# Placing query-projection pieces, two stray tiles and a ring's slots in a latent-attention kernel

## The chip, the cores and the metric

One core of a Trainium2 chip runs the whole kernel. The metric is device time in microseconds (us) of one execution; the time before is the median of 3 runs. The engines are named as in the profile: PE (TensorE, matrix products), DVE (VectorE), ACT (ScalarE), POOL (GpSimd) and SP (SyncE, which here only issues DMAs). They run side by side, each through its own queue in order, and wait for one another through semaphores.

## The reference

One layer over 2048 tokens of width 512: multi-head latent attention with 16 heads, a residual and a layer norm, then one linear layer with a second residual and norm.

```
cq   = rms_norm(x @ w_qa.T)                      # 384 wide
q    = cq @ w_qb.T                               # 16 heads, 128 nope + 64 pe
q_pe = q_pe * cos + rotate_half(q_pe) * sin
ckv  = x @ w_kva.T                               # 128 latent + 64 pe
k_pe = rope(ckv[128:]);  kv = rms_norm(ckv[:128]) @ w_kvb.T   # k_nope, v
s    = (q . k) * 192**-0.5, causal
out  = softmax(s) @ v @ w_o.T
x    = layernorm(x + out);  x = layernorm(x + x @ (w * scale).T + bias)
```

## The kernel before

Everything that enters a product in float32 is split into a high part h and a rest l, so that three products of the fast kind (hh, hl, lh) stand for one exact product. The key projection is folded into the query weights, and values are taken from the 128-wide latent itself.

The queries are four blocks b of 512 rows. A block has eight pairs p of heads, a pair has four query tiles qt of 128 rows, and a tile has two heads j. In blocks 1 to 3 a pair thus has eight head steps, numbered 2 * qt + j, from 0 to 7. The keys of a tile are nk = (4b + qt + 1) * 128, so steps get longer with qt and b.

One head step (`head_scores`, `head_probs`) is a chain over the engines. PE forms the scores s into PSUM (L407: three products with Kn, two with Kp). DVE adds the mask (L413), takes the row maximum (L440) and makes the bias (L447, L449). ACT takes the exponential into pr (L455). DVE inverts the sums; ACT writes the high half of the probabilities hl (L476) and DVE the rest (L479). SP issues a DMA that transposes hl into the ring (L483). From there PE multiplies with the latent (`values`, L532), in two halves per tile. This product is called PV in the text. ACT copies its result into ot (L537), which SP sends to memory (L292).

PSUM holds the scores in pool "s" (three buffers in blocks 1 and 3, two in block 2, which has a small pool "t" beside it) and everything else in pool "m", two buffers in turn: PV results and projection pieces. Each block has its own score pools, on the same banks.

The queries of the next pair are made in pieces between the steps: `project_pe` has two pieces of nine products (L334), one for each half x of the rope dimensions, after which DVE multiplies with cos and sin (L339), POOL combines (L346, L347), ACT rounds (L349, the tile ph), and sixteen small operations lay out pe (L358 or L360, and L361). `project_nope` has two pieces (L377), each followed by a split on ACT and DVE (L66, L67). `project_pe` serves two pairs, so pairs with even p carry four pieces (for a later pair) and those with odd p two. The weights have one buffer each: `load_wq` and `load_wpe` are issued on SP right after the last piece that reads the buffer, and must wait for it.

In blocks 1 to 3 the orders of PE and SP are the program's own; the other engines' orders come from a scheduler. A step is written as: scores of this head with the probabilities of the head before it between them, then `fill()` where a piece is due (it takes the next one from the list `fillers`), then `run_values(lag)`, which does PV halves of tiles that are far enough behind. Which steps have a piece is decided here:

```
early = b == 1 and p + 1 < NPAIR
if j != early or qt == 0 and (early or b == 2 and p > 0):
    fill()
```

The ring is 24576 columns wide. `room` finds a place for a tile's transposed probabilities: it looks only at slots of equal size, 2048 * (b + 1) columns, and while none is free it does PV halves of the oldest tiles. Block 0's last tile lies in a tile of its own, named carry, and its PV is done at step 0 of pair (1,0), by two calls of `half_values`.

After block 3 comes the output part (L775 and later), which the change leaves as it is.

Of the kernel before, what the change touches and what calls it, by code (L numbers as in the profile page):

```python
# [9 lines left out]
F16 = mybir.dt.float16  # L10
# [9 lines left out]
P = 128  # L20
# [5 lines left out]
NB = 4  # L26
QB = 512
NPAIR = H // 2
# [21 lines left out]
def mla_block(ctx: ExitStack, tc: tile.TileContext, a, out):  # L50
# [6 lines left out]
    def move(queue, dst, src):  # L57
        queue.dma_start(dst.bitcast(F32), src.bitcast(F32))
# [53 lines left out]
    prj = ctx_p.enter_context(tc.tile_pool(name="prj", bufs=1, side="right"))  # L112
# [59 lines left out]
    def value_output(p, wvo, wv, wo, pool, tag):  # L172

        for j in range(2):
            ps = pool.tile([P, HID], F32, tag=tag, name=f"ps_wo{2 * p + j}")
            nc.tensor.matmul(ps, wv[j], wo[j], start=True, stop=True)  # L176
            split(ps, wvo[:, 0, j, :], wvo[:, 1, j, :], kvln_o)
            yield
# [109 lines left out]
    def put_in(all=False):  # L288
        kept = []
        for n, dst, src in later:  # L290
            if n == 0 or all:
                nc.sync.dma_start(dst, src)  # L292
            else:
                kept.append([n - 1, dst, src])
        later[:] = kept
# [20 lines left out]
    def load_wpe(b, g):  # L316
        if b == NB:
            return
        w = state["wpe", b, g] = prj.tile([P, 2, LT, 256], F32R, tag="wpe", name=f"wpe{b}_{g}")
        move(state["queue"], w, wpe_d[g])  # L320

    def project_pe(b, g, direct=None):

        if direct is None and ("wpe", b, g) not in state:
            load_wpe(b, g)
        w = state.pop(("wpe", b, g)) if direct is None else direct
        cq, cs = state["cq"], state["cs"]
        prod = prj.tile([P, 2, 2, QB], F32, tag="prod", name=f"prod{b}_{g}")
        for x in range(2):
            ps = psum["m"].tile([P, QB], F32, tag="m", name=f"ps_pe{b}_{g}_{x}")  # L330
            n = 0
            for lt in range(LT):
                for i, k in ((0, 0), (0, 1), (1, 0)):
                    nc.tensor.matmul(  # L334
                        ps, w[:, i, lt, x * P : (x + 1) * P], cq[:, k, lt, :], start=n == 0, stop=n == 8
                    )
                    n += 1
            for k in range(2):
                nc.vector.tensor_tensor(prod[:, k, x, :], ps, cs[:, k ^ x, :], ALU.mult)  # L339
            if x:  # L340
                if b or g == 3:
                    load_wpe(*((b, g + 1) if g < 3 else (b + 1, 0)))
            yield
        rp, tp = prod[:, 0], prod[:, 1]
        eng = nc.vector if (b, g) == (0, 0) else nc.gpsimd
        eng.tensor_tensor(rp[:, 0, :], rp[:, 0, :], rp[:, 1, :], ALU.subtract)  # L346
        eng.tensor_tensor(rp[:, 1, :], tp[:, 0, :], tp[:, 1, :], ALU.add)  # L347
        ph = prj.tile([P, 2, QB], F32R, tag="ph", name=f"ph{b}_{g}")
        nc.scalar.activation(ph, rp, AF.Copy)  # L349
        pe = blk.tile([P, 4, QB], F32R, tag="pe", name=f"pe{b}_{g}")  # L350

        quick = b == 0 or g == 0
        for j in range(4):
            q = slice(32 * j, 32 * j + 32)
            for x in range(2):
                to = pe[32 * x : 32 * x + 32, j, :]
                if quick:
                    nc.scalar.activation(to, rp[q, x, :], AF.Copy)  # L358
                else:
                    nc.gpsimd.tensor_copy(to, rp[q, x, :])  # L360
                (nc.gpsimd if not quick or (b, g) == (0, 0) and j % 2 else nc.vector).tensor_tensor(  # L361
                    pe[64 + 32 * x : 96 + 32 * x, j, :], rp[q, x, :], ph[q, x, :].bitcast(F32), ALU.subtract
                )
        state["pe", b, g] = pe

    def project_nope(b, p, direct=None):
        if direct is None and ("wq", b, p) not in state:
# [22 lines left out]
    def project(b, p):  # L390
        if p % 2 == 0:
            yield from project_pe(b, p // 2)
        yield from project_nope(b, p)
# [191 lines left out]
    for _ in project_pe(0, 0, wpe0):  # L585
        pass
# [13 lines left out]
    probs, vals = [], []  # L600

    def flush():
        while probs:
            for _ in probs.pop():
                pass

    def units(pool, ring, b):
        lag = min(ring.shape[1] // (2048 * (b + 1)) - 1, 3)

        for p in range(NPAIR):  # L610
            put_in(True)
            if b and p % 2 == 0 and p + 2 < NPAIR:
                fillers.append(project_pe(b, p // 2 + 1))
            if p + 1 < NPAIR:
                fillers.append(project(b, p + 1) if b == 0 else project_nope(b, p + 1))
            elif b + 1 < NB:
                fillers.append(project(b + 1, 0))
            if b == NB - 1 and p == NPAIR - 2:
                wv = state["wv"] = blk.tile([P, H, P], F32, tag="pe", name="wv")
                nc.sync.dma_start(wv, a["wv"])  # L620
                wo = state["wo"] = [pool.tile([P, 4, HID], F32, tag="wo", name="wo0", bufs=1)]
                nc.sync.dma_start(wo[0], a["wo"][:, 0:4])
            if b == NB - 1 and p == NPAIR - 1:
                ctx_p.close()
                pcr = state["pcr"] = ctx.enter_context(
                    tc.tile_pool(name="pcr", bufs=2, side="right", reuse_waits="tile")
                )
                wvo = state["wvo"] = [pcr.tile([P, 2, 2, HID], F32R, name=f"wvo{p}", bufs=1) for p in range(2)]
                wv, wo = state["wv"], state["wo"]
                for i in range(2):  # L630
                    fillers.append(
                        value_output(
                            i, wvo[i], [wv[:, 2 * i + j] for j in range(2)], [wo[0][:, 2 * i + j] for j in range(2)],
                            psum["m"], "m",
                        )
                    )
                wo.append(blk.tile([P, 4, HID], F32, tag="qn", name="wo1"))
                nc.sync.dma_start(wo[1], a["wo"][:, 4:8])
            for qt in range(4):
                nk = (4 * b + qt + 1) * P  # L640
                if (b, p, qt) == (0, NPAIR - 1, 3):
                    s0, PT = -4 * nk, prj.tile([P, 4 * nk], F16, tag="prod", name="carry")
                else:
                    s0 = room(2048 * (b + 1), ring.shape[1])
                    PT = ring[:, s0 : s0 + 4 * nk]
                vg = values(b, p, qt, nk, PT)
                if nk <= 512:
                    pi = pair_scores(pool, b, p, qt, nk)
                    flush()
                    probs.append(pair_probs(pool, b, p, qt, nk, PT, *pi))  # L650
                    fill()
                    next(side[0], None)
                    if p and qt % 2:
                        next(side[1], None)
                    if qt % 2:
                        next(side[0], None)
                    run_values(lag)
                    run_values(lag)
                else:
                    for j in range(2):  # L660
                        prev = probs.pop() if probs else iter(())
                        pi = head_scores(pool, b, p, j, qt, nk, prev)
                        probs.append(head_probs(pool, b, p, j, qt, nk, PT, *pi))
                        if (b, p, qt, j) == (1, 0, 0, 0):
                            half_values()
                            half_values()
                        early = b == 1 and p + 1 < NPAIR
                        if j != early or qt == 0 and (early or b == 2 and p > 0):
                            fill()
                        run_values(lag)  # L670
                vals.append([vg, 0, s0, s0 + 4 * nk])
            drain()
# [7 lines left out]
    def run_values(depth):  # L680

        for _ in range(1 + len(vals) - depth):
            half_values()

    def room(n, size):

        while True:
            for c in range(0, size - n + 1, n):
                if all(c + n <= v[2] or c >= v[3] for v in vals):
                    return c  # L690
            if len(vals) == 1:
                flush()
            half_values()
# [20 lines left out]
    ring = blk13.tile([P, 12 * 2048], F16, name="ring", bufs=1)  # L714
# [202 lines left out]
```

## Time and profile before

| | |
|---|---|
| median of 3 runs | 1661.89 us (1661.62 to 1665.02) |
| profiled execution | 1661.02 us, its span 1659.2 us |
| mean granted TensorE clock | 0.981 |
| PE busy | 1567.8 us, 94% |
| DVE busy | 1172.6 us, 71% |
| ACT busy | 936.1 us, 56% |
| POOL busy | 330.7 us, 20% |
| block 1's first scores / end of block 3 | about 257 us / 1393 us from the start |
| pair (1,3), pair (2,3), pair (3,3) | 30.7, 42.8, 58.1 us |

A row of the list of waits reads: who waited, for whom, us in total, how many times, the longest. A row of a stretch reads: start and end, length, busy time of each engine with its number of instructions, granted TensorE clock, share of the time that the DMA engines were busy, GB/s. A row of the timeline reads: start, duration, engine, line, operation, output and inputs, number merged, and in brackets the idle time before it with what ended it. A row of a group of instructions ends in its busy time, the mean in ns, and the engine's idle time before it.

### The profile page before, as it was taken

Reading aid. Unit: us, or ns where it says so; the run is one execution under the profiler, and the core shown is the slowest. Engines: PE = TensorE matmul, PEld = TensorE weight load, DVE = VectorE, ACT = ScalarE, POOL = GpSimd, SP = SyncE. Lnnn points to the kernel's source line nnn. Section 1 sums busy time; section 2 is a strip of 40 time slices with the busy share of each in tenths; the row PEclk is TensorE's granted clock in tenths of the full one; section 3 lists DMA queues with packets and bytes.
Section 4 is the critical chain, followed back from the end, with each engine's and each line's share of the span. In section 5 each row is a group of like instructions: output and inputs, shape, how many; then the busy total and the mean of one; then the engine's idle time right before and its main releaser. Section 6 shows DMA issues by size and latency. Waiting matters only on the chain. (4 is left out here: it accounts for less than half of the span.)

```text
span 1659.2 us, 24718 instructions
## 1 busy us (share of the span) xinstructions
PE 1567.8 (94%) x9130; PEld 1299.4 (78%) x9130; DVE 1172.6 (71%) x2115; ACT 936.1 (56%) x1647; POOL 330.7 (20%) x404
## 2 busy tenths in 40 slices
PE   8998997999998799999998999999999997999997
PEld 7787876778777678888887888888888785788886
DVE  6777776777777868787786777767767774455464
ACT  5776765565556646666675656666566664312120
POOL 2332424143100505040000310500500000022132
PEclk9999998999999999999999999999999998999999
DMA  6979674878787767878887677787688998333230
GB/s 218 246 213 238 156 194 108 165 163 159 159 193 151 146 141 149 178 153 169 201 180 140 117 160 153 152 159 161 126 158 191 189 179 188 105 108 120 90 121 32
DMA packets 632841, 262.50 MB, mean 158 GB/s; under 512 B 570288, under 2 KB 611120, under 8 KB 631696
## 3 DMA queue, kind: packets, MB, share of 16 engines
q1 hardware_dynamic: 621184, 233.35, 64.7%
q0 software_dynamic: 4768, 17.99, 3.5%
q10 hardware_dynamic: 6768, 9.57, 1.9%
q8 instruction: 72, 1.18, 0.3%
q14 instruction: 49, 0.40, 0.1%
HBM read 83.17 MB, written 35.13 MB: 71 GB/s over the span
## 5 line engine op out<-in xcount | busy, mean ns | idle before, releaser
L407 PE MATMUL s<-Kn,qn 128*128 128x512 f32 (+4 forms) x1920 | 520.7, 377 | 12.2 <-ACT pr L455 10.3
L455 ACT ACTIVATE pr<-s,bias,rq 128x1024 f32<-128x1024 f32 (+3 forms) x320 | 324.1, 1016 | 194.2 <-DVE bias L449 150.4
L532 PE MATMUL o<-ring,V 128*128 128x256 f16 x3252 | 400.7, 277 | 27.7 <-DMA ring<-hl 18.2
L479 DVE SCALAR_TENSOR_TENSOR hl<-pr,inv,hl 128x1024 f16<-128x1024 f32 (+7 forms) x320 | 358.7, 1136 | 83.0 <-ACT hl L476 81.2
L532 PEld LDWEIGHTS <-V 128*128 128x128 f16 x3264 | 307.4, 99 | 117.6 <-issue 61.6
L476 ACT ACTIVATE hl<-pr,inv 128x1024 f16<-128x1024 f32 (+7 forms) x320 | 295.4, 961 | 182.6 <-DMA ring<-hl 74.9
L407 PEld LDWEIGHTS s<-Kn,qn 128*128 128x128 f32 x1920 | 338.7, 190 | 61.1 <-ACT pr L455 16.6
L440 DVE TENSOR_REDUCE neg<-s 128x1 f32<-128x1024 f32 (+3 forms) x320 | 318.5, 995 | 83.9 <-PE s L407 79.9
L407 PE MATMUL s<-Kp,pe 128*128 128x512 f32 (+4 forms) x1280 | 361.0, 363 | 0.0
L407 PEld LDWEIGHTS s<-Kp,pe 128*128 128x128 f32 x1280 | 234.0, 189 | 29.8
L377 PE MATMUL ps_qn<-cq,wq 128*128 128x512 f32 x576 | 151.9, 410 | 23.0 <-DMA wq<-wq_d 15.5
L346 POOL TENSOR_TENSOR prod<-prod 128x512 f32<-128x512 f32 x15 | 19.3, 1288 | 740.7 <-DVE prod L339 740.7
L377 PEld LDWEIGHTS ps_qn<-cq,wq 128*128 128x128 f32 x576 | 111.1, 198 | 47.6 <-issue 12.5
L775 PE MATMUL acc<-wvo,oh 128*128 128x512 f32 x448 | 143.5, 401 | 0.0
L361 POOL TENSOR_TENSOR pe<-prod,ph 32x512 fp32r<-32x512 f32 x76 | 119.7, 1575 | 10.0 <-issue 5.1
L775 PEld LDWEIGHTS acc<-wvo,oh 128*128 128x128 f32 x448 | 83.4, 188 | 20.9 <-issue 2.9
L775 PE MATMUL acc<-wvo,ol 128*128 128x512 f32 x224 | 88.4, 395 | 0.0
L284 POOL DMA_DIRECT2D ot_d<-ot x33 | 18.7, 568 | 293.8 <-ACT ot L537 263.1
L334 PE MATMUL ps_pe<-cq,wpe 128*128 128x512 f32 x288 | 73.2, 400 | 2.3 <-DMA cq<-cq_d 1.6
L537 ACT ACTIVATE ot<-o 128x256 f32<-128x256 f32 x128 | 48.0, 376 | 38.0 <-PE o L532 36.3
L63 ACT ACTIVATE oh<-o 128x1024 fp32r<-128x1024 f32 x28 | 29.6, 1058 | 67.6 <-PE acc L775 53.5
L64 DVE TENSOR_TENSOR ol<-o,oh 128x1024 fp32r<-128x1024 f32 x28 | 38.5, 1376 | 41.3 <-ACT oh L63 41.3
(140 smaller groups left out, 1624.3 us busy)
## 6 DMA issues: line engine op xcount, KB each, us to landing
wq<-wq_d SPq DMA_DIRECT2D x22, 768.0 KB, 5.6
o<-ot_d SPq DMA_DIRECT2D x32, 512.0 KB, 3.3
ot_d<-ot SPq DMA_DIRECT2D x95, 128.0 KB, 2.4
wpe<-wpe_d SPq DMA_DIRECT2D x10, 768.0 KB, 4.8
wq<-wq_d POOLq DMA_DIRECT2D x9, 768.0 KB, 6.2
wq_d<-wst SPq DMA_DIRECT2D x9, 512.0 KB, 4.7
cq_d<-cqst SPq DMA_DIRECT2D x18, 256.0 KB, 3.6
ot_d<-ot POOLq DMA_DIRECT2D x33, 128.0 KB, 2.6
```

The lines of the kernel that those rows point to most:

```text
L64: nc.vector.tensor_tensor(l, ps, h.bitcast(F32), ALU.subtract)
L334: nc.tensor.matmul(ps, w[:, i, lt, x * P : (x + 1) * P], cq[:, k, lt, :], start=n == 0, stop=n == 8)
L361: (nc.gpsimd if not quick or (b, g) == (0, 0) and j % 2 else nc.vector).tensor_tensor(pe[64 + 32 * x : 96 + 32 * x, j, :], rp[q, x, :], ph ...
L377: nc.tensor.matmul(ps, w[:, i, lt, j * P : (j + 1) * P], cq[:, k, lt, :], start=n == 0, stop=n == 8)
L407: nc.tensor.matmul(ps[:, :w], lhs, K[:, i, c0 : c0 + w], start=n == 0, stop=n == 4)
L440: nc.vector.tensor_reduce(neg[:, ti : ti + 1], v, axis=AX.XY, op=ALU.max, negate=True)
L455: nc.scalar.activation(pr[:, c0 : c0 + n * w].rearrange("p (a c) -> p a c", a=n), v, AF.Exp, bias=bias, scale=r, accum_out=sums[:, ti : ti ...
L476: nc.scalar.activation(hl[:, 0, c], pr[:, c], AF.Copy, scale=inv)
L479: nc.vector.scalar_tensor_tensor(hl[:, 1, c], pr[:, c], inv, hl[:, 0, c], ALU.mult, ALU.subtract)
L532: nc.tensor.matmul(ps[:, :256], vt[:, i, k % 4, :], v[:, :, l, k, :], start=n == 0, stop=n == 3 * kts - 1)
L537: nc.scalar.activation(ot, ps[:, :256], AF.Copy)
L775: nc.tensor.matmul(acc, l[:, t, c], wvo[p][:, i, j, :], start=p == 0 and j == 0 and n == 0, stop=p == NPAIR - 1 and j == 1 and n == 2,)
```

## The change

The steps that carry a piece become a table `at`: 0, 1, 3, 4 in pairs with four pieces (0, 1, 2, 3 in (1,0)), 3, 4 in pairs with two, 1, 2, 4, 5 in the last pair of blocks 1 and 2, and 1, 3, 5, 7 in the last pair of block 3. In `project_pe` the work after the products (combining, rounding, laying out) follows the second piece at once; before, it was done with the next piece. The laying out of pe for (2,0) and (3,0) goes from ACT and DVE to POOL, as that of the other groups of blocks 1 to 3. The carry tile takes the buffer of tag "ph" in place of "prod", and its PV is done at step 2 of (1,0). `room` may also place a tile right behind a live one, in just the width that it needs: when no slot is free, or first of all for the last three tiles of block 2.

```diff
@@ project_pe
             for k in range(2):
                 nc.vector.tensor_tensor(prod[:, k, x, :], ps, cs[:, k ^ x, :], ALU.mult)
-            if x:
-                if b or g == 3:
-                    load_wpe(*((b, g + 1) if g < 3 else (b + 1, 0)))
-            yield
+            if x == 0:
+                yield
+            elif b or g == 3:
+                load_wpe(*((b, g + 1) if g < 3 else (b + 1, 0)))
...
-        quick = b == 0 or g == 0
+        quick = b == 0 or (b, g) == (1, 0)
...
         state["pe", b, g] = pe
+        yield
@@ units
             put_in(True)
+            if p + 1 == NPAIR:
+                at = (1, 2, 4, 5) if b < NB - 1 else (1, 3, 5, 7)
+            elif p % 2 == 0 and p + 2 < NPAIR:
+                at = (0, 1, 2, 3) if (b, p) == (1, 0) else (0, 1, 3, 4)
+            else:
+                at = (3, 4)
...
-                    s0, PT = -4 * nk, prj.tile([P, 4 * nk], F16, tag="prod", name="carry")
+                    s0, PT = -4 * nk, prj.tile([P, 4 * nk], F16, tag="ph", name="carry")
                 else:
-                    s0 = room(2048 * (b + 1), ring.shape[1])
+                    s0 = room(2048 * (b + 1), ring.shape[1], 4 * nk, (b, p) == (2, NPAIR - 1) and qt > 0)
...
-                        if (b, p, qt, j) == (1, 0, 0, 0):
+                        if (b, p, qt, j) == (1, 0, 1, 0):
                             half_values()
                             half_values()
-                        early = b == 1 and p + 1 < NPAIR
-                        if j != early or qt == 0 and (early or b == 2 and p > 0):
+                        if 2 * qt + j in at:
                             fill()
@@ room
-    def room(n, size):
+    def room(n, size, need, dense):
         while True:
-            for c in range(0, size - n + 1, n):
-                if all(c + n <= v[2] or c >= v[3] for v in vals):
+            slots = [(c, n) for c in range(0, size - n + 1, n)]
+            gaps = [(c, need) for c in sorted([0] + [v[3] for v in vals]) if c + need <= size]
+            for c, w in gaps + slots if dense else slots + gaps:
+                if all(c + w <= v[2] or c >= v[3] for v in vals):
                     return c
```

## The prediction

> **What bounds the kernel now.** I read the page first, then TensorE's waits, then granted clock by stretch, then the timeline around the longest waits. TensorE (PE) is the bound: busy 94% of the span, with 91 us of idle. The change touches only the stretch from block 1's first scores (257 us) to the end of block 3 (1393 us), so I asked for PE's waits there (columns: total us, number of waits, longest):
>
> ```profile
> PE ps_qn L377 <- DMA wq<-wq_d: 15.0, 3, 11.5
> PE s L407 <- ACT pr L455: 10.3, 13, 2.3
> PE o L532 <- DMA ring<-hl: 8.5, 5, 4.3
> PE ps_qn L377 <- DVE qn L67: 5.0, 4, 2.3
> PE o L532 <- DMA carry<-hl: 5.0, 1, 5.0
> PE o L532 <- ACT ot L537: 3.8, 4, 2.7
> PE o L532 <- DVE prod L339: 0.9, 1, 0.9
> PE ps_pe L334 <- DVE prod L339: 0.8, 2, 0.4
> ```
>
> They add up to 49.3 us, all of TensorE's idle time there; nothing else can be won except clock. The clock is the second loss. Rows below: stretch, its length, PE busy, granted clock, DMA share, GB/s.
>
> ```profile
> 570.00:626.00 56.00, 44.47 (x266) 0.91 0.65 137
> 672.60:715.20 42.60, 42.60 (x267) 1.00 0.82 160
> 264.80:270.40 5.60, 5.60 (x20) 0.50 0.38 82
> 424.00:427.40 3.40, 3.26 (x11) 0.50 0.63 116
> 366.40:369.80 3.40, 3.40 (x20) 1.00 0.94 190
> 584.20:587.90 3.70, 3.66 (x9) 0.51 1.22 261
> 903.20:908.70 5.50, 5.50 (x27) 0.50 1.02 203
> ```
>
> The first two are the same work (an odd pair of block 2, heads of 1152 to 1536 keys): 56.0 us with the wait for wq, 42.6 us without. The others follow a wait: after 5.0, 2.34, 11.5 and 4.3 us of idle TensorE runs at half clock for some us, after 2.27 us (366.40) it does not. Half of a stretch at half clock is lost time.
>
> Why the longest wait exists, from the timeline (start, duration; SPq is the DMA queue of SP):
>
> ```profile
> 566.16 2.24 PE L377 MATMUL ps_qn<-cq,wq 128*128 128x512 f32 x9
> 574.72 3.61 SPq L483 DMA_TRANSPOSE ring<-hl  x1
> 578.42 0.56 SPq L58 DMA_DIRECT2D wq<-wq_d  x1
> 584.24 3.99 PE L377 MATMUL ps_qn<-cq,wq 128*128 128x512 f32 x9 [11.53 <-DMA wq<-wq_d]
> ```
>
> The single wq buffer is free at 568.4, but its reload stands on SP behind a transposition whose input comes at 574.7; it is issued at 578.4 and lands 5.7 us later. The next piece had been placed only one head after.
>
> **The change, part by part.** Work and matmuls are the same (9130); it moves them. I name a head step by its place in a pair, 0 to 7, and a pair (block, pair).
>
> 1. *Projection pieces at chosen steps.* Pieces stood at steps 0, 1, 2, 4 (block 1, even pairs), 0, 1, 3, 5 (block 2), 1, 3, 5, 7 (block 3), and 0, 1 or 1, 3 in odd pairs. They go to 0, 1, 3, 4 and 3, 4. From the last q_nope piece of one pair to the first of the next there are now 7 steps where (2,0) to (2,1) had one and (1,0) to (1,1) four. In the changed program the wq load stands on SP before the transposition of step 4, which is ready later than the piece, so nothing is held up behind it; it has some 20 us or more for a landing of 5 to 6 us. All three wq waits go: 11.53 + 2.75 + 0.71 = 15.0 us, and with them 3.7 and 3.4 us at half clock, that is 1.85 + 1.7. Gain 18.6. The cq, cs and wpe loads move on SP too: cq2 and cs2, landed 9.8 us after issue (471.2 to 481.0), go from step 1 to step 4 of (1,6) and are wanted 5 steps (some 17 us) later; covered.
> 2. *PSUM of the pieces.* Two pieces in a row at steps 0 and 1 of a pair reuse a buffer that ACT and DVE must first empty: the four "DVE qn" waits. At 3 and 4 the buffers between come from PV tiles, emptied by one ACT copy with a score of 2.1 us or more as cover. Gain 5.0; what is late next is that copy, which I charge under 7.
> 3. *Carry.* Block 0's last PV moves from step 0 to step 2 of (1,0). Two scores and two pieces, some 8 us, go first; the transposition lands at 264.7 and the new place comes at about 268. The idle 4.97 and 5.6 us at half clock (2.8) go: 7.8. The tile shares the buffer of ph now, so ACT's ph of pair 1 waits for that PV; in the built order it stands behind the PV's own copy, and its other input (POOL, 2.6 us after step 1's piece) is no earlier. Nothing.
> 4. *Rope copies of q_pe for (2,0) and (3,0) go to POOL.* ACT loses 8 copies of 628 ns (5.0 us), DVE 8 subtractions of 684 ns (5.5 us), in (1,7) where DVE is busy 31.5 of 38 us and its reduction trails the score by 6 us. That lag and the piece at step 7 are behind 2.74 (ot), 1.05, 0.37 and 0.90 us of waits and 1.4 us of clock. With (1,5)'s 2.34 + 1.7, where a lone piece at step 4 leaves three bare steps, the gain is 10.5. POOL pays 8 x 0.77 + 8 x 1.58 + 2.6 = 21.4 us; the first score of (2,0) waits for the second subtraction only, about 14 us after the piece, and 22 us of TensorE work lie between. **A rule against it:** DVE's hl subtraction over 896 keys takes 1152 ns in a pair without POOL and 1403 in one with it:
>
> ```profile
> L479 DVE SCALAR_TENSOR_TENSOR hl<-pr,inv,hl 128x896 f16<-128x896 f32 x2 | 2.3, 1152 | 2.9 <-ACT hl L476 2.9
> L479 DVE SCALAR_TENSOR_TENSOR hl<-pr,inv,hl 128x896 f16<-128x896 f32 x3 | 4.2, 1403 | 3.1 <-ACT hl L476 3.1
> ```
>
> The Trainium skill, "SBUF — State Buffer", section "SBUF: two separate sides", has GpSimd and a two-input VectorE operation hold one port pair in turn, the loser blocked for the whole instruction. By the row some 6 subtractions under the burst lose 0.25 to 0.55 us each, about 2.5 us against 5.5 saved; by the rule up to 1.58 each, 9.5 us, and DVE would be worse off. I take the row, and charge 0.6 for what reaches TensorE.
> 5. *Last tiles of block 2 packed.* Before, (3,0)'s first slot needed two PV tiles forced out early:
>
> ```profile
> 893.75 5.09 PE L532 MATMUL o<-ring,V 128*128 128x256 f16 x45
> 897.71 0.79 ACT L455 ACTIVATE pr<-s,bias,rq 128x512 f32<-128x512 f32 x1
> 903.16 6.47 PE L532 MATMUL o<-ring,V 128*128 128x256 f16 x33 [4.32 <-DMA ring<-hl]
> ```
>
> The wait of 4.32 and 5.5 us at half clock (2.75) go: 7.1. But this PV was a cover. In the changed program (3,0)'s first score comes right after 15 of those 45 matmuls, about 895.5, and waits for the last exp of block 2 (the ACT row, ended 898.5): a new wait of 3.0 us, between 1 and 4 as the softmax trails, and long enough for the clock, 1.7. Cost 4.7.
> 6. *New waits of the same kind at (2,0):* its first two scores need the exps of the last two heads, with one PV (1.1 us) as cover instead of 3.3. Cost 2.0.
> 7. *Six bare steps.* Even pairs end bare at 5, 6, 7, odd ones begin bare at 0, 1, 2: twelve stretches. In block 1 a score needs the exp three heads back; six bare steps stood in odd pairs before, and that exp came 0.35 to 1.65 us in time at their end. Now the last three are short heads (2.7 us apart, not 3.2), so 1.4 us less: 0.75 in each of block 1's four, 3.0. Block 2 had 2 us or more to spare, block 3 settled at 0.3 to 0.6 in bare steps: 1.0 for both. (1,0) and (1,1), with DVE 22.9 of 26 us and no PV at steps 4 and 5: 2.5.
>
> Gains 18.6 + 5.0 + 7.8 + 10.5 + 7.1 = 49.0; costs 0.6 + 4.7 + 2.0 + 3.0 + 1.0 + 2.5 = 13.8; net 35.2. The profiled execution took 1661.0 us (span 1659.2), so 1625.8; the median stands 0.9 above it: 1627.
>
> **The clock rule.** The skill's "TensorE: Matmul & The Clock Gate", section "HAM oscillation — how this bites in real kernels", puts the limit at idle gaps over some 3.4 us. The rows show half clock after 2.34 to 2.75 us. By the rule the waits of 2.34, 2.74 and 2.75 would cost no clock (4.8 us less gain) and the new 3.0 us at (3,0) none either (1.7 less cost): net 32 instead of 35. I follow the rows.
>
> **The rivals.**
> *Bubbles come back (0.18).* The waits are a symptom of a softmax and a DMA that are nearly full (DMA share 0.82 in an undisturbed pair); each of twelve bare stretches waits 1.6 us, short of the clock: 19 us, less the 4 charged: 1642; with late PV inputs besides, 1648. For: scores of block 1 had 0.14 us to spare at several pair ends. Against: block 2's four middle pairs have no idle at all.
> *Slower (0.10): bare stretches cross the clock's limit.* If each of the twelve waits 2.5 us, half clock follows, 1.7: 50 us less 4, 1673. It decides from about 3.2 us a stretch, clock included. Against: the six bare steps before never waited.
> *It does not do what it says (0.02):* another queue entry holds the loads up as long, waits stay: 1662.
> The forecast has 0.70.
>
> **How the numbers follow.** The forecast's costs could be 5 (waits at block starts covered) or 25, so 1613 to 1641; the first rival reaches to 1653. Range 1612 to 1653. About 0.2% is what a measurement of this kernel can tell from no change. Faster 0.88, within it 0.02, slower 0.10.
>
> **What would show it.** Right: no PE wait for wq or carry; "DVE qn" near 0; pair (2,1) about 43 us; PE idle from block 1 to 3 near 15 to 25 us. New: the first score of (3,0) waiting 2 to 4 us for ACT pr, with half clock after it. Wrong: many "s <- ACT pr" waits over 2 us at steps 0 to 2 of odd pairs, or q_pe waited for from POOL at (2,0).

## The result and the profile after

The changed kernel took 1647.54 us (median of 4 runs, 1646.49 to 1648.62), the kernel before 1663.08 us beside it (1661.62 to 1665.02): ratio 0.9901, 95% interval 0.9885 to 0.9917. It is faster, by 15.5 us where 35.2 were forecast; the time lies in the range and on the rival "Bubbles come back" (1642 to 1648). The profiled execution took 1647.43 us, its span 1645.3, mean clock 0.988.

TensorE's waits between 257 and 1380 us, as shown of before:

```profile
PE s L408 <- ACT pr L456: 26.5, 25, 3.6
PE o L533 <- DMA ring<-hl: 6.1, 5, 4.5
PE ps_pe L334 <- DMA cq<-cq_d: 3.1, 1, 3.1
PE o L533 <- DVE qn L67: 0.6, 1, 0.6
PE o L533 <- ACT ot L538: 0.5, 1, 0.5
```

36.8 us against 49.3, where the prediction named 15 to 25 as the sign of being right. The rows for wq (15.0), carry (5.0) and qn at ps_qn (5.0) are gone; ACT pr, the exponential, has gone from 10.3 us in 13 waits to 26.5 in 25, and one wait for cq is new.

Where the time went, block by block, from the starts of each block's first scores in the two traces:

| stretch | before | after | idle PE before, after | PE busy at half clock before, after |
|---|---|---|---|---|
| block 1 | 268.5 | 254.0 | 21.3, 10.5 | 15.1, 3.4 |
| block 2 | 384.0 | 360.8 | 19.5, 4.9 | 9.2, 3.4 |
| block 3 | 483.7 | 506.6 | 8.3, 21.4 | 0.0, 11.3 |
| everything else | 522.9 | 523.9 | | |

(The idle time ahead of a block's first score is put to the new block, but its length to the old one. The half clock that begins at 871.2, 1.2 us ahead of block 3's first score, is put to block 3. The half clock that runs at block 1's first score in both, some 3 us, is left out.) Of block 2's 23.2 us, 7.1 are only moved: 63 PV matmuls of its last tile, which the old `room` forced out early, are now done in block 3. So blocks 1 and 2 won 30.6 us and block 3 gave 15.7 back.

Pair (3,3) before:

```profile
1088.00:1146.00 58.00, 58.00 (x360) 48.23 (x358) 40.74 (x62) 36.49 (x54) 0.00 (x0) 1.00 0.82 164
```

Stretches of after: pairs (2,1), (2,3) and (3,3), then four that bear on the clock (columns: PE, weight loads, DVE, ACT and POOL, the others as before):

```profile
557.40:600.70 43.30, 43.08 (x267) 36.18 (x266) 34.31 (x68) 31.80 (x57) 0.00 (x0) 1.00 0.90 172
646.40:689.00 42.60, 42.60 (x267) 36.09 (x266) 33.73 (x67) 29.80 (x55) 0.00 (x0) 1.00 0.87 161
1061.90:1121.80 59.90, 58.50 (x360) 48.21 (x358) 42.55 (x63) 37.27 (x54) 0.00 (x0) 1.00 0.76 150
446.00:451.40 5.40, 3.65 (x24) 2.96 (x23) 3.48 (x7) 3.78 (x6) 0.00 (x0) 1.00 0.46 107
451.40:454.80 3.40, 3.40 (x12) 3.21 (x11) 1.79 (x7) 1.45 (x3) 0.00 (x0) 0.51 1.05 210
476.00:484.00 8.00, 4.88 (x30) 3.98 (x29) 3.13 (x8) 1.18 (x3) 0.00 (x0) 1.00 1.18 200
871.20:878.00 6.80, 5.64 (x15) 4.68 (x16) 4.71 (x7) 3.13 (x6) 0.00 (x0) 0.50 0.77 111
```

Pair (2,1) fell from 56.0 to 43.3 us, as foreseen. Pair (3,3) rose from 58.0 to 59.9. Pairs 1 to 5 and 7 of block 3 each wait 1.4 us, as it does.

The timeline shows why wq is no longer waited for:

```profile
578.95 7.64 SPq L484 DMA_TRANSPOSE ring<-hl  x2
580.47 2.24 PE L378 MATMUL ps_qn<-cq,wq 128*128 128x512 f32 x9
587.30 0.54 SPq L58 DMA_DIRECT2D wq<-wq_d  x1
619.90 2.22 PE L378 MATMUL ps_qn<-cq,wq 128*128 128x512 f32 x9
```

The reload still stood 4.6 us on SP after the piece had ended (582.7), behind transpositions, as it did before; the prediction had nothing holding it up. What changed is the next use, 32.6 us after the issue instead of 5.8.

At the end of block 2, the answer to the packing:

```profile
866.95 1.81 PE L533 MATMUL o<-ring,V 128*128 128x256 f16 x15
871.45 0.76 ACT L456 ACTIVATE pr<-s,bias,rq 128x512 f32<-128x512 f32 x1
872.36 1.65 PE L408 MATMUL s<-Kn,qn 128*128 128x512 f32 x3 [3.59 <-ACT pr L456]
```

The two forced PV halves and the 4.32 us wait are gone, and the first score of (3,0) waits 3.59 us for the last exponential of block 2. It then runs at half clock: 6.8 us with a granted clock of 0.50, in the row 871.20 above.

### The profile page after: what moved, and what is told of

Same layout as the page of the kernel before. It is cut to its first block, busy times and chain, and to the rows that moved or that the text cites. A ratio compares the mean times of both kernels' runs of the same rounds, so it can differ in the third digit from the quotient of the medians.

```text
span 1645.3 us, 24717 instructions
## 1 busy us (share of the span) xinstructions
PE 1563.1 (95%) x9130; PEld 1295.0 (79%) x9130; DVE 1162.4 (71%) x2099; ACT 928.4 (56%) x1631; POOL 361.7 (22%) x436
## 5 line engine op out<-in xcount | busy, mean ns | idle before, releaser
L408 PE MATMUL s<-Kn,qn 128*128 128x512 f32 (+4 forms) x1920 | 524.6, 379 | 28.4 <-ACT pr L456 26.5
L477 ACT ACTIVATE hl<-pr,inv 128x1024 f16<-128x1024 f32 (+7 forms) x320 | 295.4, 961 | 172.5 <-DMA ring<-hl 69.8
L378 PE MATMUL ps_qn<-cq,wq 128*128 128x512 f32 x576 | 145.9, 398 | 0.7 <-ACT ot L538 0.3
L361 POOL TENSOR_TENSOR pe<-prod,ph 32x512 fp32r<-32x512 f32 x92 | 141.6, 1539 | 11.0 <-issue 5.1
L468 DVE TENSOR_SCALAR inv<-sums 128x1 f32<-128x1 f32 x128 | 26.9, 210 | 78.3 <-ACT pr L456 78.2
L538 ACT ACTIVATE ot<-o 128x256 f32<-128x256 f32 x128 | 48.0, 376 | 59.9 <-PE o L533 59.9
L66 ACT ACTIVATE qn<-ps_qn,kvln 128x512 fp32r<-128x512 f32 x64 | 43.7, 684 | 51.1 <-PE ps_qn L378 51.0
```

The source lines that it names most:

```text
L66: nc.scalar.activation(h, ps, AF.Copy, scale=scale)
L378: nc.tensor.matmul(ps, w[:, i, lt, j * P : (j + 1) * P], cq[:, k, lt, :], start=n == 0, stop=n == 8)
L408: nc.tensor.matmul(ps[:, :w], lhs, K[:, i, c0 : c0 + w], start=n == 0, stop=n == 4)
L477: nc.scalar.activation(hl[:, 0, c], pr[:, c], AF.Copy, scale=inv)
L538: nc.scalar.activation(ot, ps[:, :256], AF.Copy)
```

## The experiments

All kernels below start from the changed kernel unless said otherwise. Ratios are to the kernel before, run beside them, so that the changed kernel's own 0.9901 is the mark. The theory: block 3 pays because VectorE's order there is different, and because pair (3,6) meets the weights of the output part at the wrong moment. The rival: six bare steps are as such too long for block 3, whatever the order.

**Block 3 with its old steps.**

```diff
             else:
                 at = (3, 4)
+            if b == NB - 1:
+                at = (1, 3, 5, 7)
```

> The changed kernel, with the pieces of block 3 alone put back at steps 1, 3, 5, 7 (even pairs) and 1, 3 (odd pairs would get 1, 3 too, since they have two pieces). If the gain of blocks 1 and 2 was given back by where block 3's pieces stand, block 3 (first score of (3,0) to its last PV but one) falls from 506.5 to about 496 us and the time from 1647.5 to about 1637. If block 3 is longer for another reason (packing, clock), it stays at 1647.

Measured 1636.06 us, ratio 0.9813 (0.9791 to 0.9835). Block 3 took 497.0 us instead of 506.6, and its pairs 1 to 5 waited 0.5 to 1.7 us each. So the new steps of block 3 cost time. This does not yet say whether bareness or order is the reason.

**VectorE in program order in block 3.** In the changed kernel VectorE's order comes from the scheduler. In a bare step of an odd pair of the kernel before, VectorE ran (start, duration):

```profile
1137.16 1.23 DVE L440 TENSOR_REDUCE neg<-s 128x1 f32<-128x1024 f32 x1 [0.91 <-PE s L407]
1138.31 1.21 DVE L479 SCALAR_TENSOR_TENSOR hl<-pr,inv,hl 128x960 f16<-128x960 f32 x1
1139.43 0.27 DVE L449 TENSOR_SCALAR bias<-neg,rq 128x1 f32<-128x1 f32 x1
1139.62 1.21 DVE L479 SCALAR_TENSOR_TENSOR hl<-pr,inv,hl 128x960 f16<-128x960 f32 x1
```

The same work after the change:

```profile
1111.82 1.22 DVE L441 TENSOR_REDUCE neg<-s 128x1 f32<-128x1024 f32 x1 [1.04 <-PE s L408]
1112.96 2.34 DVE L480 SCALAR_TENSOR_TENSOR hl<-pr,inv,hl 128x960 f16<-128x960 f32 x2
1115.22 0.27 DVE L450 TENSOR_SCALAR bias<-neg,rq 128x1 f32<-128x1 f32 x1
```

Before, the bias of a head stood between the two halves of the previous head's subtraction; now it stands behind both. The exponential waits for the bias, which now starts one subtraction later: 2.26 us after the subtractions begin instead of 1.12. The experiment leaves the steps as they are and changes only the order:

```diff
-                units(blk13, ring, b)
+                if b == NB - 1:
+                    with tc.manual_schedule(engines={mybir.EngineType.DVE}):
+                        units(blk13, ring, b)
+                else:
+                    units(blk13, ring, b)
```

> The changed kernel, with VectorE of block 3 in the program's own order in place of the scheduler's: each head's bias then stands between the two halves of the subtraction for the head before it. If the order is what makes the exps late, the waits of 0.9 and 0.5 us that stand in every pair of block 3 go (some 10 us over eight pairs) and the time is about 1638 to 1641, with pair (3,6) still waiting. If it is the lack of pieces in the bare steps itself, the waits stay and the time is 1647. If a fixed order makes VectorE wait behind the pieces' operations, it is slower: 1655 or more.

Measured 1633.59 us, ratio 0.9797 (0.978 to 0.9813). The same work once more, and the stretch of pair (3,3), again with six bare steps ahead of its two pieces and three behind them:

```profile
1109.28 0.27 DVE L450 TENSOR_SCALAR bias<-neg,rq 128x1 f32<-128x1 f32 x1
1109.47 1.21 DVE L480 SCALAR_TENSOR_TENSOR hl<-pr,inv,hl 128x960 f16<-128x960 f32 x1
```

```profile
1059.30:1117.10 57.80, 57.80 (x360) 48.35 (x358) 42.75 (x64) 37.13 (x54) 0.00 (x0) 1.00 0.78 155
```

Idle in pairs 1 to 5 is zero, pair (3,3) takes 57.8 us against 59.9, and block 3 487.0 against 506.6. The rival falls: bare steps cost these pairs nothing when the bias comes in time. The order costs 2.1 us in each of pairs 1 to 5, of which the list of waits shows 1.4. The rest stands in the profile as busy time (58.50 us against 57.80), in the matmuls at these waits. Of block 3's 19.6 us, 10.4 came from pairs 1 to 5, 4.4 from (3,6) and 3.7 from (3,0).

**Pair (3,6) with its old steps.**

```diff
+            if (b, p) == (NB - 1, NPAIR - 2):
+                at = (1, 3)
```

> The changed kernel, with only pair (3,6)'s two pieces back at steps 1 and 3. Its waits of 4.5 us (transposed probabilities) and 3.5 us (exp) shrink to the 0.6 and 1.3 us of before, and two stretches at half clock go: 1647.5 to about 1639. If the loads of wv and wo hold the transposition whatever the pieces do, the 4.5 us stay and the time is about 1643.

Measured 1640.12 us, ratio 0.9834 (0.9813 to 0.9854). Block 3 took 502.3 us; the pair's idle time fell from 8.9 to 5.0. The wait for the transposition was still 2.8 us, so the steps are only a part of this pair's loss.

**The output part's weights later.** Ahead of the 4.5 us wait in pair (3,6), the timeline of after shows on SP the loads of wv and wo, 1 MB each, and then the transposition that TensorE waits for:

```profile
1252.56 0.38 SPq L629 DMA_DIRECT2D wv<-in_wv_dram  x1
1252.99 0.45 SPq L631 DMA_DIRECT2D wo<-in_wo_dram  x1
1253.96 21.11 SPq L484 DMA_TRANSPOSE ring<-hl  x3
1267.82 4.11 PE L533 MATMUL o<-ring,V 128*128 128x256 f16 x24 [4.49 <-DMA ring<-hl]
```

The row merges three transpositions. TensorE needs the first, which landed at 1267.78, 13.8 us after its issue. In the kernel before it landed 11.0 us after its issue beside the same loads, a piece stood at step 1 ahead of this PV, and TensorE waited 0.63 us. The experiment puts the loads behind the transpositions of step 0:

```diff
-            if b == NB - 1 and p == NPAIR - 2:
-                wv = state["wv"] = blk.tile([P, H, P], F32, tag="pe", name="wv")
-                nc.sync.dma_start(wv, a["wv"])
-                wo = state["wo"] = [pool.tile([P, 4, HID], F32, tag="wo", name="wo0", bufs=1)]
-                nc.sync.dma_start(wo[0], a["wo"][:, 0:4])
...
                         probs.append(head_probs(pool, b, p, j, qt, nk, PT, *pi))
+                        if (b, p, qt, j) == (NB - 1, NPAIR - 2, 0, 1):
+                            wv = state["wv"] = blk.tile([P, H, P], F32, tag="pe", name="wv")
+                            nc.sync.dma_start(wv, a["wv"])
+                            wo = state["wo"] = [pool.tile([P, 4, HID], F32, tag="wo", name="wo0", bufs=1)]
+                            nc.sync.dma_start(wo[0], a["wo"][:, 0:4])
```

> The changed kernel with the loads of wv and of wo's first half (1 MB each) issued in step 1 of pair (3,6), behind the transpositions of step 0, instead of at the head of the pair. If these loads are what stretches the transposition that PE waits 4.5 us for, that wait shrinks to 1 us or less and the half-clock window behind it goes: 4 to 6 us faster than the changed kernel, ratio about 0.987. If the bare steps at the head of the pair are the cause and the loads are not, the wait stays at 3 us or more and the time at 1646 to 1648 us, ratio 0.990. If the loads then come late for what follows block 3, the projection of values starts later and the time after block 3 grows beyond its 266 us.

Measured 1639.63 us, ratio 0.9849 (0.9822 to 0.9875).

```profile
1249.08 9.91 SPq L484 DMA_TRANSPOSE ring<-hl  x2
1258.30 2.79 PE L533 MATMUL o<-ring,V 128*128 128x256 f16 x24
1259.09 0.53 SPq L670 DMA_DIRECT2D wv<-in_wv_dram  x1
```

The wait is gone (the PV's row has none in brackets), the first transposition landed 8.3 us after its issue instead of 13.8, and the pair fell from 69.8 to 65.2 us; the part after block 3 stayed at 267 us. So the loads stretched the transposition, and the bare steps made that visible. The pair's other wait (3.5 us at 1301.76) stayed. Its timeline in after:

```profile
1296.57 1.22 DVE L64 TENSOR_TENSOR ol<-o,oh 128x1024 fp32r<-128x1024 f32 x1 [1.26 <-ACT oh L63]
1298.96 1.22 DVE L64 TENSOR_TENSOR ol<-o,oh 128x1024 fp32r<-128x1024 f32 x1 [0.17 <-ACT oh L63]
1300.11 0.27 DVE L450 TENSOR_SCALAR bias<-neg,rq 128x1 f32<-128x1 f32 x1
1301.76 1.65 PE L408 MATMUL s<-Kn,qn 128*128 128x512 f32 x3 [3.50 <-ACT pr L456]
```

The scheduler had put two splits of the output part ahead of a bias. With program order in block 3 this wait was 2.0 us, so the order is behind a part of it.

**Only the wq part, in the kernel before.**

```diff
+                        if (b, p) == (2, 0):
+                            due = 2 * qt + j in (0, 1, 3, 4)
+                        elif (b, p) == (2, 1):
+                            due = 2 * qt + j in (3, 4)
+                        else:
+                            due = j != early or qt == 0 and (early or b == 2 and p > 0)
+                        if due:
                             fill()
```

> The kernel before, with one thing changed: pieces at steps 0, 1, 3, 4 in pair (2,0) and 3, 4 in (2,1), so that the wq load is queued seven steps ahead there. By the prediction's row it gains the whole wait, 11.5 us, and half of 3.7 us at half clock: 13.4 us, ratio 0.992. If the wait only moves (the loads land late at the new place, or bare steps wait instead), 5 us or less: 0.997 or more.

Measured 1655.57 us beside 1664.62, ratio 0.9948 (0.9933 to 0.9963): 8.7 us. Block 2 fell from 384.0 to 372.9, that is 11.1, where the prediction's share for this one wait is 11.53 + 1.85 = 13.4; a new "DVE qn" wait of 1.8 us in (2,0) and 1.3 us more at its first score account for 3.1, more than the 2.3 that are missing.

**The carry tile at its old place and in its old buffer.**

```diff
-                    s0, PT = -4 * nk, prj.tile([P, 4 * nk], F16, tag="ph", name="carry")
+                    s0, PT = -4 * nk, prj.tile([P, 4 * nk], F16, tag="prod", name="carry")
...
-                        if (b, p, qt, j) == (1, 0, 1, 0):
+                        if (b, p, qt, j) == (1, 0, 0, 0):
```

> The changed kernel, with the carry tile back in the buffer of prod and its PV at step 0 of (1,0). By the prediction 7.8 us slower than the changed kernel (wait 5.0, half of 5.6 us at half clock), ratio 0.995 against 0.990. If the pieces at the new steps had covered the landing anyway, no difference: 0.990.

Measured 1656.12 us, ratio 0.995 (0.9933 to 0.9967): about 8 us slower than the change as it is, and the intervals don't meet. The wait for the carry is back, 4.7 us; block 1 took 257.4 us, against 249.4 to 254.0 in the seven traces with the carry as in the change and block 1 otherwise the same.

**The rope copies on ACT and DVE again.**

```diff
-        quick = b == 0 or (b, g) == (1, 0)
+        quick = b == 0 or g == 0
```

> The changed kernel, with the laying out of pe for (2,0) and (3,0) back on ACT and DVE. If GpSimd slows VectorE as in the trace row (0.25 to 0.55 us for each subtraction that it meets), putting it back costs some 3 to 6 us in (1,7) and (2,0): ratio 0.992 to 0.994 against 0.990. If GpSimd blocked VectorE for whole instructions, putting it back would gain: 0.987 or less.

Measured 1654.07 us, ratio 0.9946 (0.993 to 0.9962), about 7 us slower by the ratios; in the profiled runs blocks 1 and 2 together grew by 2.8 (617.7 us against 614.9). Single executions scatter: in the five other traces that leave both blocks alone they took 610.7 to 616.4 us. The sign is shown, the size lies between 3 and 7.

**No packing.**

```diff
-    s0 = room(..., 4 * nk, (b, p) == (2, NPAIR - 1) and qt > 0)
+    s0 = room(..., 4 * nk, False)
```

> The changed kernel without the packing of block 2's last tiles: the forced PV, its wait and its half clock come back, the 3.6 us wait at the first score of (3,0) goes. By the prediction's sum (7.1 against 4.7) 2.4 us slower: 1650. If the new wait costs what the old one did, no change: 1647.5.

Measured 1652.92 us beside 1666.74, ratio 0.9908 (0.9876 to 0.994): no difference clear of noise. Blocks 2 and 3 together took 869.5 us in its profiled run against 867.4. But the old wait of 4.3 us did not come back: the forced PV waited 0.6, the first score of (3,0) not at all, and 3.2 and 1.1 us of waiting for the exponential turned up at steps 3 and 4 of (3,0). The lag at the end of block 2 is paid in one of these places.

**The last pieces of (1,6) earlier, for the cq load.**

```diff
+            if (b, p) == (1, NPAIR - 2):
+                at = (0, 1)
```

> The changed kernel, with the two pieces of pair (1,6) at steps 0 and 1, so that the loads of block 2's cq and cs are queued three steps earlier. The wait of 3.1 us for cq in (1,7), which the prediction had called covered, goes; four bare steps come behind it (2 to 7 of (1,6)). Expected 2 to 3 us faster than the changed kernel: ratio 0.988 to 0.989. If two pieces in a row at steps 0 and 1 wait for VectorE as before (1.1 us) and the bare steps wait as well, no difference.

Measured 1646.26 us, ratio 0.9892 (0.9876 to 0.9909): no difference. The wait for cq (3.1) is gone; in its place stand 1.1 us for wq, 1.0 for a transposition, 1.7 for an inverse on DVE and 2.3 for qn.

**A piece as cover at the blocks' ends.**

```diff
-                at = (1, 2, 4, 5) if b < NB - 1 else (1, 3, 5, 7)
+                at = (1, 2, 5, 7) if b < NB - 1 else (1, 3, 5, 7)
```

> The changed kernel with the pieces of the last pairs of blocks 1 and 2 at steps 1, 2, 5, 7 instead of 1, 2, 4, 5, so that one piece of 2.1 us stands right ahead of the first score of the next block. If the 3.1 and 3.6 us at the first scores of (2,0) and (3,0) are simply bare steps, that is exp and PE's work out of balance, each shrinks to about 1 to 1.5 us, together 4 us, and the half-clock window behind the second goes (1.7 us): ratio 0.987 to 0.988. If the pieces moved are missed where they stood, the waits turn up at step 4 of those pairs and the time stays at 1646 to 1648 us.

Measured 1650.66 us, ratio 0.9914 (0.9888 to 0.9939): a miss. The wait at (2,0) fell from 3.1 to 1.5 us, but 1.4 turned up at step 5 of (1,7) and 1.4 in (2,0). The wait at (3,0) was 3.7 us, not smaller: measured from block 2's first score, the scores of its last head ended 2.0 us earlier than in after, the last exponential ended no earlier, and TensorE, with the piece behind those scores, was at the wait when it had been before. There the softmax trails, and not for want of scores.

**VectorE in program order in all three blocks.**

```diff
-    with tc.manual_schedule(engines={mybir.EngineType.PE, mybir.EngineType.SP}):
+    with tc.manual_schedule(engines={mybir.EngineType.PE, mybir.EngineType.SP, mybir.EngineType.DVE}):
```

> The changed kernel with VectorE in the order in which the program issues its work in blocks 1 to 3 (in the earlier run only in block 3, 1633.6 us, ratio 0.980). If the late bias is the cause in block 1's bare odd pairs too, the seven or so waits of 1.2 to 1.7 us there go as well: 2 to 8 us below the earlier run, ratio 0.975 to 0.979. The rival: elsewhere the scheduler's order is the better one, because the program's order lets VectorE stand at an operation whose input is late while ready work is behind it; then block 1 or block 2 grows by what block 3 gained, ratio 0.980 to 0.99.

Measured 1664.06 us, ratio 1.0005 (0.9991 to 1.002): the whole gain is gone, worse than the rival had it. The timeline of (1,7) shows how:

```profile
481.55 1.28 DVE L480 SCALAR_TENSOR_TENSOR hl<-pr,inv,hl 128x1024 f16<-128x1024 f32 x1 [6.95 <-ACT hl L477]
490.24 1.29 DVE L339 TENSOR_TENSOR prod<-ps_pe,cs 128x512 f32<-128x512 f32 x2
491.58 1.65 PE L533 MATMUL o<-ring,V 128*128 128x256 f16 x7 [6.52 <-DVE prod L339]
```

In program order VectorE stood 6.95 us at a subtraction whose input was late (ACT's hl waited for a transposition), and the product that empties the PSUM of a piece done at 479.7 came only at 490.2. TensorE waits for "DVE prod" came to 19.1 us where after has none, and block 2 took 391.9 us. Block 3, with the same order, took 488.9.

**Both repairs together.** Program order in block 3 only, and the later loads.

> The changed kernel with both repairs that held alone: VectorE in program order in block 3 only (1633.6 us, ratio 0.980), and the loads of wv and wo's first half behind the transpositions of step 0 of pair (3,6) (1639.6 us, ratio 0.985). If the two waits are separate, the gains add: block 3 loses its 1.4 us per pair and the 4.5 us before o3_5_3, 17 to 20 us below the changed kernel's 1647.5, that is 1627 to 1631 us, ratio 0.975 to 0.979. If the transposition was late only because VectorE's order made its input late as well, the second repair adds nothing and the time stays at 1633 to 1634 us, ratio 0.980.

Measured 1621.95 us beside 1665.73, ratio 0.9743 (0.9723 to 0.9762). It beats both kernels and lies below both expectations. The repairs add: alone they take 0.0104 and 0.0052 off the ratio of the change, together 0.0158. Pair (3,6) fell to 59.9 us, block 3 to 483.0. The row of TensorE's waits for the exponential, between 262 and 1372 us:

```profile
PE s L408 <- ACT pr L456: 16.2, 10, 4.2
```

Two of these waits, 4.2 us at (2,0) and 3.6 at (3,0), are the blocks' ends, which no experiment removed without a new wait elsewhere.

## Why the prediction was right in its sign and wrong in its size

The waits that the change was made to remove went, and blocks 1 and 2 won most of what was forecast. The step that failed is step 7, for block 3: it put the bare steps of blocks 2 and 3 together at 1.0 us, and block 3, with its first score, lost 18.7 us where 5.7 were charged. What the runs showed in its place: the new steps also changed the scheduler's order on VectorE, and with program order there block 3 fell from 506.6 to 487.0 us; with the loads of wv and wo moved as well it took 483.0. The loss of block 3 is 13.0 of the 19.7 us that are missing; the other 6.7 lie in blocks 1 and 2. In the prediction's own terms, with idle time and half of PE's busy time at half clock, from the table above:

| | predicted | measured |
|---|---|---|
| blocks 1 and 2 (steps 1 to 5, less 0.6, 2.0, 3.0 and 2.5) | 40.9 | 25.5 idle + 8.7 clock = 34.2 |
| block 3 and its first score (4.7 + 1.0) | -5.7 | -13.0 idle - 5.7 clock = -18.7 |

(The lengths above gave 30.6 and -15.7: there the 3.6 us ahead of block 3's first score count to block 2.)

- *Step 1, wq:* right in the waits, 15.0 us gone, and the one-part kernel shows that this single wait carries 9 to 11 us. Its sentence that cq2 and cs2 are "covered" failed: TensorE waited 3.1 us for cq at step 1 of (1,7).

```profile
459.73 2.23 PE L378 MATMUL ps_qn<-cq,wq 128*128 128x512 f32 x9
468.76 0.62 SPq L58 DMA_DIRECT2D cq<-cq_d  x1
480.02 2.32 PE L334 MATMUL ps_pe<-cq,wpe 128*128 128x512 f32 x9 [3.12 <-DMA cq<-cq_d]
```

  The load stood 6.8 us on SP after the piece, behind two transpositions, and landed 11.1 us after its issue; TensorE came 14.9 us after the piece. The experiment that moved the load earlier showed that this slack is shared, since other waits took its place.
- *Step 2, qn:* right; no such wait is left at ps_qn.
- *Step 3, carry:* right; predicted 7.8, putting it back cost about 8.
- *Step 4, rope copies:* right in sign; the experiment gives 3 to 7 us for the copies, the prediction 10.5 together with (1,5), where waits of 0.34 and 1.26 us for the exponential stand in place of the 2.34. The row weighed there gave the right sum, but the rule behind it, that GpSimd and a two-input VectorE operation hold a port pair in turn, is what (1,7) shows too. VectorE's subtractions before:

```profile
L479 DVE SCALAR_TENSOR_TENSOR hl<-pr,inv,hl 128x896 f16<-128x896 f32 x2 | 2.3, 1147 | 0.2 <-ACT hl L476 0.2
L479 DVE SCALAR_TENSOR_TENSOR hl<-pr,inv,hl 128x768 f16<-128x768 f32 x2 | 2.0, 1018 | 2.6 <-ACT hl L476 2.6
```

and after, with POOL's 16 operations beside them, then one of these subtractions with the two of POOL that it meets:

```profile
L480 DVE SCALAR_TENSOR_TENSOR hl<-pr,inv,hl 128x896 f16<-128x896 f32 x3 | 4.1, 1359 | 1.4 <-ACT hl L477 1.4
L480 DVE SCALAR_TENSOR_TENSOR hl<-pr,inv,hl 128x768 f16<-128x768 f32 x2 | 3.4, 1737 | 0.1
507.76 1.26 POOL L361 TENSOR_TENSOR pe<-prod,ph 32x512 fp32r<-32x512 f32 x1
508.18 1.78 DVE L480 SCALAR_TENSOR_TENSOR hl<-pr,inv,hl 128x896 f16<-128x896 f32 x1
509.08 2.01 POOL L361 TENSOR_TENSOR pe<-prod,ph 32x512 fp32r<-32x512 f32 x1
```

  3 x 0.21 + 2 x 0.72, with 2 x 0.15 for the two of 640 keys, makes 2.4 us, where the row had given 2.5. The single instructions tell why. The one at 508.18 begins with 0.84 us of POOL's left to run and takes 0.63 longer than alone (1.15); the POOL one behind it begins 0.89 before VectorE ends and takes 0.75 longer than its neighbour. In the 14 traces 474 subtractions begin while such a POOL subtraction runs: each is longer than alone by what that one has left, less 0.2 us (by nothing where less is left), to within 0.01 us; on average 0.60. So VectorE waits for the running instruction of POOL to end, as the rule has it. The 9.5 us were a bound that this trace does not come near: they charged six whole instructions, but only the rest of the one that is running is lost. That putting the copies back cost time, where the expectation of that run has a gain under such blocking, is no sign against it.
- *Step 5, packing:* the old wait went and the foreseen new one came: 3.6 us, predicted 3.0, and the half clock behind it cost half of 5.7 us, 2.8, instead of 1.7. The price was 6.4 instead of 4.7; taking the packing away made no measurable difference.
- *Step 6, (2,0):* 3.1 us against 1.05 before, predicted 2.0 more. Right.
- *Step 7, bare steps:* block 1's odd pairs but the last, and (1,6), waited 1.2 to 1.7 us each for the exponential, 5.8 in all, and another 1.6 for transpositions in the same bare steps, against 5.5 predicted. Block 2 waited for nothing in its middle. For block 3 the step failed: against the 1.0 charged to blocks 2 and 3, pairs 1 to 5 and 7 took 6.0 us more than before (370.6 against 364.6) and (3,6) 9.1 more (69.8 against 60.7). The prediction read block 3's spare time of "0.3 to 0.6" from the trace of before, as if VectorE's order were fixed. That order is the scheduler's, and it changed with the steps; the experiment with program order took these waits away without touching a step. In (3,6) it overlooked the two loads on SP and the output's splits on VectorE, whose cost the old steps had largely hidden.
- *The clock:* 12.2 us were forecast to be won in blocks 1 and 2 (1.85 + 1.7 + 2.8 + 1.4 + 1.7 + 2.75); 8.7 were. Half clock came behind a bare step of (1,6) (451.4) and behind the 3.1 us wait at (2,0) (512.8), 1.7 us each; neither had been charged. Block 3, without half clock before, lost 5.7. The prediction judged each wait by its length; the traces show another rule (last section).

The rival "Bubbles come back" had the right time by luck, with another reason. It put 1.6 us on twelve bare stretches; block 2's show none, and block 3's come from order and loads.

What stays open: why the scheduler put the bias behind both halves, and what would remove the lag of the softmax at the ends of blocks 1 and 2.

## What to carry to other kernels

When pieces of work move on an engine with a fixed order, compare the order of the engines that a scheduler fills too: spare time read from the old trace holds only for the old order. Fixing an engine's order helps where its inputs arrive in that order, and hurts where one late input holds ready work behind it, so try it by stage. And before work that covered a stretch is taken away, list every DMA and every operation of the next stage that starts there.

## What the runs showed of the hardware

The half clock follows a grid in time, not single gaps. In the clock records of 14 profiled runs, the half-clock stretches of a run begin at whole multiples of 3.413 us from one another: in after at 451.4, 512.8, 871.2 and 1267.1, which are 18, 105 and 116 such steps apart. Its phase differs from run to run. Summing TensorE's idle time within each window of this grid between 250 and 1390 us: all 81 windows that were followed by a change to half clock had 1.75 us idle or more, and only 10 windows with 1.75 to 1.98 us were not followed by one, none with more. So about 1.9 us of 3.4, wherever in the window, decides. Once the clock is halved, less is enough to keep it so: of the windows at half clock 76 were followed by another, all with 0.62 us idle or more, and 38 were not, all with 0.77 or less.

The rows of after show both sides. Before 451.4 two gaps of 0.51 and 1.24 us fell into one window and the next ran at 0.51. The 3.12 us gap that ended at 480.02 was cut by the grid at 478.7 into 1.8 and 1.3 us, and the row 476.00 has the full 1.00. Both windows lie at the lower edge, where either was seen; what they show is that the length of a single gap does not decide. The Trainium skill, "TensorE: Matmul & The Clock Gate", section "HAM oscillation — how this bites in real kernels", has gaps over some 3.4 us as the limit; by these runs a gap of 2 us can be enough, and one of 3 can be free. The price of a wait of 2 to 3.4 us is thus a matter of chance: of 41 such waits in these runs 16 had no half clock, 22 had one window of it (1.3 to 1.7 us lost) and 3 had two (3.0 to 3.1).
